# Paired heads in scores and values, a group normalisation kept in transposed layout, and a longer planned time for GpSimd's inverse roots

## The chip, the cores and the metric

The kernel runs on one core of a Trainium2 chip. Its time is the device time of one execution in microseconds (us). Three executions took 18460.33, 18463.09 and 18468.82 us; the median, 18463.09 us, is the time before.

A core has TensorE (PE in the profile; its weight loads are PEld), VectorE (DVE), ScalarE (ACT), GpSimd (POOL) and SyncE (SP), whose queue here issues all DMAs. Every engine works through its own instruction stream in order and waits on semaphores for the others.

## What is computed

32 audio sequences of 160000 samples are cut into 313 frames of 512 samples (S = 313, width 512) and turned by a cosine transform. One layer follows: an attention part and a feature part, each behind a layer norm and added to its input.

```
h = frames @ dct.T                                  # 32 x 313 x 512
X = layernorm(h)
Q, K = xpos(X @ W_Q), xpos(X @ W_K);  V = X @ W_V   # 8 heads of 64
p = softmax(Q @ K.T) * gamma_h ** |n - m|
Y = p @ V
Yn = per head: (Y - mean) * rsqrt(var + 1e-5), then * gn_weight + gn_bias
h = h + (silu(X @ W_G) * Yn) @ W_O
X = layernorm(h)
theta = X[..., None, :] / (1 + |W|) + B             # 256 x 512 angles for each frame
h = h + silu(sum_d(cos(theta) * a_cos) @ P_cos + sum_d(sin(theta) * a_sin) @ P_sin)
```

The sines and cosines are read from a table of 4096 angles in the reference; the kernel rounds the angle to the same 4096 steps and lets ScalarE compute the sine.

## The kernel before

**The feature part** is the bulk. In `ffn_round`, sequences go through it in pairs; up to four pairs form a ring, and each pair stays for 8 rounds of 32 features. `STARTS` lists the round in which each of the 16 pairs joins: pair 0 at round 0 alone, pair 1 at round 4, pair 2 at 7, pair 3 at 9, pair 4 at 11, and so on; from round 11 on the ring mostly holds three or four pairs, at the end one. A slot is 24 feature-by-sequence parts (7512 columns): VectorE makes the indices (L620, one instruction for each feature and 128 dimensions over all sequences of the ring, then L629 and L636 over the slot), ScalarE takes two sines of each slot (L644, tile `trig`, 2 buffers), TensorE sums them over the dimensions with one-hot weights of 32 columns in four column groups (L666). With one pair in the ring a slot needs 12 instructions on L620, with four pairs 3.

**The attention part** (`attention`) prepares a sequence for the ring. The frames of a sequence lie in NT = 3 overlapping tiles of N = 105 rows (`ROW0` = 0, 104, 208). Sequences 0 and 1 are prepared side by side in two sets of buffers, A and B, before the first feature round. From then on set A alone prepares the others, one after the other, beside the feature rounds, and also serves `output`. Each set has one PSUM tile `W` of four banks.

The steps of one attention are:

- `rows` (L288, 512-wide products), `copy`, `layernorm` (its inverse root is `rsqrt`: a seed on VectorE, L230 and L233, and three Newton steps of four instructions on GpSimd, L239 to L242; its result is used in L263), `transposed` (L275).
- `rows` for V into `x.h`, `rotary` for two heads at a time (`columns`, L303; L368 and L371 on VectorE; `x.qk` holds two heads in partitions 0 to 63 and 64 to 127).
- `scores`, one head at a time: three matmuls (L382) into banks 0, 1 and 2, one maximum over 105x939 (L390), one subtraction (L393).
- `exps` on ScalarE. With eng = "DVE" the sums of the exponentials follow on VectorE; with eng = "ACT" ScalarE accumulates them. "ACT" is used for sequences 0 and 1 and where the ring has one pair or none.
- For each head: the transpose of the exponentials (L436, banks 0 to 2), the decay (L448, with a window of the decay table loaded into `x.u`), the product with V (L454, nine matmuls of 105x105 by 105x64 into bank 3, in three issues); after each second head the copy back into `x.h` (L468).
- The gate (`columns` into all four banks), `silu` on ScalarE out of them (L478).
- The group normalisation in frame-by-frame layout: squares (L486 on ScalarE or L489 on VectorE), sums over each head of 64 (L494), L496 to L499 for the sums of the softmax, `rsqrt`, L503, the product (L506), then the transposes (L275), weight and bias (L517), the product with the gate (L522).
- `rows` with W_O, the residual (L525), `layernorm`, `transposed`, `copy`, and the store of the normalised sequence, transposed, to DRAM (L533). The feature rounds load it from there (L604).

**The order of the instructions** is made by `Plan`. Every step is added with a key, an engine, a planned duration and what it reads and writes. `emit` simulates the engines with these durations (300 ns more between engines, 2500 ns for a DMA to land) and issues, on each engine, the ready step with the smallest key. Feature steps have keys that count ScalarE activations of a whole slot; an attention gets keys spread between two of these, in proportion to `SHARE`, so that it is to be ready 8 such activations ahead of the round that needs it. The planned durations fix only the order; on the chip each instruction waits for what it needs. `rsqrt` plans 7500 ns for GpSimd's part.

## Time and profile before

The profiled execution took 18458.81 us, 4.28 us under the median; its span, from the first instruction to the last, is 18457.0 us.

| what | busy us | share of the span |
|---|---|---|
| ACT, of it L644 (2758 sines) | 17389.6 | 94% |
| ACT, all else | 428.2 | 2% |
| DVE, of it L620, L636, L629 | 15012.4 | 81% |
| DVE, all else | 2176.8 | 12% |
| PE, of it L666 | 10225.0 | 55% |
| POOL, all | 1128.9 | 6% |

A busy share is an average over stages. The view by stretches, cut where the ring changes, shows which engine is full in each; it is the one to read first. The view of waits says for each engine what ended its idle time, the view of groups gives the number and mean duration of like instructions, and the timeline lists instructions in order with the idle time before them in brackets.

### The profile page before, as it was taken

Reading aid. Unit: us, or ns where it says so; the run is one execution under the profiler, and the core shown is the slowest. Engines: PE = TensorE matmul, PEld = TensorE weight load, DVE = VectorE, ACT = ScalarE, POOL = GpSimd, SP = SyncE. Lnnn points to the kernel's source line nnn. Section 1 sums busy time; section 2 is a strip of 40 time slices with the busy share of each in tenths; the row PEclk is TensorE's granted clock in tenths of the full one; section 3 lists DMA queues with packets and bytes.
Section 4 is the critical chain, followed back from the end, with each engine's and each line's share of the span. In section 5 each row is a group of like instructions: output and inputs, shape, how many; then the busy total and the mean of one; then the engine's idle time right before and its main releaser. Section 6 shows DMA issues by size and latency. Waiting matters only on the chain. (4 is left out here: it accounts for less than half of the span.)

```text
span 18457.0 us, 326424 instructions
## 1 busy us (share of the span) xinstructions
PE 14446.5 (78%) x148768; PEld 6739.2 (37%) x148768; DVE 17189.2 (93%) x11340; ACT 17817.8 (97%) x3246; POOL 1128.9 (6%) x1222
## 2 busy tenths in 40 slices
PE   8888888887887887887888788877877777766666
PEld 4443434333333333333333333333333333322222
DVE  6999999999999999999999999999999999988888
ACT  3889999999999999999999999999999999999998
POOL 0001000000000000000000000000000000000000
PEclk8999999999999999999999999999999999988888
DMA  3222122111111111111121111111111111110102
GB/s 90 75 68 63 57 66 59 54 47 58 51 41 47 59 48 51 51 43 54 47 59 46 45 51 50 56 50 55 40 46 50 40 55 49 44 39 22 38 27 59
DMA packets 605415, 946.91 MB, mean 51 GB/s; under 512 B 118880, under 2 KB 344160, under 8 KB 593792
## 3 DMA queue, kind: packets, MB, share of 16 engines
q1 hardware_dynamic: 604032, 926.03, 16.9%
q8 instruction: 1166, 19.10, 0.4%
q14 instruction: 217, 1.78, 0.0%
HBM read 821.10 MB, written 104.66 MB: 50 GB/s over the span
## 5 line engine op out<-in xcount | busy, mean ns | idle before, releaser
L644 ACT ACTIVATE trig<-ix 128x7512 f32<-128x7512 int16 (+1 forms) x2758 | 17389.6, 6390 | 324.0 <-PE pa L666 140.3
L666 PE MATMUL pa<-trig,hot 128*32 128x313 f32 x131072 | 10225.0, 465 | 3490.1 <-ACT trig L644 3446.6
L666 PEld LDWEIGHTS pa<-trig,hot 128*32 128x32 f32 x131072 | 4261.3, 118 | 9265.0 <-ACT trig L644 4673.0
L620 DVE TENSOR_SCALAR ix<-xT,f 128x2504 int16<-128x2504 f32 (+3 forms) x5504 | 6526.4, 1245 | 93.8 <-ACT trig L644 55.9
L636 DVE TENSOR_SCALAR ix<-ix 128x15024 int16<-128x15024 int16 (+4 forms) x1655 | 5582.1, 3387 | 40.7
L629 DVE TENSOR_SCALAR ix<-ix 128x7512 int16<-128x7512 int16 (+1 forms) x1379 | 2903.9, 2106 | 551.9 <-ACT trig L644 466.6
L303 PE MATMUL a_W<-a_xnT,a_ring 128*128 128x313 f32 x4896 | 1445.6, 439 | 21.6 <-DVE a_prob L368 5.8
L288 PE MATMUL a_W<-a_ring,a_u 128*105 128x512 f32 x2256 | 1089.2, 623 | 124.1 <-DMA a_u<-in_frames 49.1
L303 PEld LDWEIGHTS a_W<-a_xnT,a_ring 128*128 128x128 f32 x4896 | 884.8, 190 | 576.0 <-issue 247.1
L239 POOL TENSOR_TENSOR a_gu<-a_gr 105x24 f32<-105x24 f32 x93 | 109.8, 1180 | 9222.8 <-DVE a_gr L233 9218.0
L288 PEld LDWEIGHTS a_W<-a_ring,a_u 128*105 128x105 f32 x2256 | 368.8, 175 | 731.0 <-issue 647.9
L454 PE MATMUL a_W<-a_h,a_prob 105*105 105x64 f32 x4464 | 487.9, 264 | 135.4 <-DVE a_prob L448 135.0
L454 PEld LDWEIGHTS a_W<-a_h,a_prob 105*105 105x105 f32 x4464 | 449.6, 177 | 268.5 <-issue 141.1
L382 PE MATMUL a_W<-a_u 64*105 64x313 f32 x1488 | 463.5, 444 | 64.0 <-DVE a_prob L393 50.6
L239 POOL TENSOR_TENSOR a_lu<-a_lr 105x3 f32<-105x3 f32 x186 | 197.8, 1063 | 4617.1 <-DVE a_lr L233 4528.9
L288 PE MATMUL a_W<-a_ring,a_xnT 128*105 128x512 f32 x744 | 355.0, 614 | 10.1 <-ACT a_xnT L223 5.4
L382 PEld LDWEIGHTS a_W<-a_u 64*105 64x105 f32 x1488 | 232.0, 169 | 294.1 <-issue 91.7
L436 PE MATMUL a_W<-ident,a_prob 105*105 105x105 f32 x2232 | 300.5, 272 | 32.0 <-ACT a_prob L408 17.9
L448 DVE TENSOR_TENSOR a_prob<-a_W,a_u 105x939 f32<-105x939 f32 x248 | 280.0, 1129 | 40.3 <-PE a_W L436 34.8
L390 DVE TENSOR_REDUCE a_mx<-a_W 105x3 f32<-105x939 f32 x248 | 280.0, 1129 | 36.2 <-PE a_W L382 36.1
L436 PEld LDWEIGHTS a_W<-ident,a_prob 105*105 105x105 f32 x2232 | 244.8, 177 | 127.4 <-issue 71.2
L393 DVE TENSOR_TENSOR a_prob<-a_W,a_mx 105x939 f32<-105x939 f32 x248 | 281.7, 1136 | 8.4
(134 smaller groups left out, 3474.1 us busy)
## 6 DMA issues: line engine op xcount, KB each, us to landing
hot<-in_hot SPq DMA_DIRECT2D x1376, 128.0 KB
xT<-xT_d SPq DMA_DIRECT2D x80, 1252.0 KB
a_u<-in_decay SPq DMA_DIRECT2D x248, 260.5 KB
xT<-xT_d SPq DMA_DIRECT2D x36, 939.0 KB
a_ring<-in_proj SPq DMA_DIRECT2D x128, 256.0 KB
a_ring<-in_dct SPq DMA_DIRECT2D x124, 256.0 KB
a_ring<-wv_d SPq DMA_DIRECT2D x124, 256.0 KB
a_ring<-in_wq SPq DMA_DIRECT2D x124, 256.0 KB
```

Source lines behind the costliest of these rows:

```text
L239: nc.gpsimd.tensor_tensor(u, r, r, ALU.mult)
L288: lambda c=c, i=i, k=k, to=to: nc.tensor.matmul(x.W[:N, to, :], lhsT[:, c, ROW0[i] : ROW0[i] + N], x.ring[k], start=(c == 0), stop=(c == N ...
L303: lambda c=c: nc.tensor.matmul(x.W[:, bank, :S], w[:, c, :], x.xnT[:, c, :], start=(c == 0), stop=(c == NC4 - 1)),
L382: lambda i=i: nc.tensor.matmul(x.W[:N, i, :S], qk[r0 : r0 + DH, 0, ROW0[i] : ROW0[i] + N], qk[r0 : r0 + DH, 1, :], start=True, stop=True,),
L393: lambda: nc.vector.tensor_tensor(x.prob[:N, hd], x.W[:N, :NT, :S], m[:N].unsqueeze(2).to_broadcast((N, NT, S)), ALU.subtract),
L436: nc.tensor.transpose(x.W[:N, jj, ROW0[i] : ROW0[i] + N], x.prob[:N, a, i, ROW0[j] : ROW0[j] + N], ident[:N, :N],)
L454: nc.tensor.matmul(x.y[:N, i, (hd % 2) * DH : (hd % 2 + 1) * DH], x.prob[:N, a, jj, ROW0[i] : ROW0[i] + N], x.h[:N, jj, hd * DH : (hd + 1) ...
L620: nc.vector.tensor_scalar(ix[:, x[0], pt * r * S : (pt + 1) * r * S], now["xT", y][:, : r * S], f[:, 0, n : n + 1], f[:, 1, n : n + 1], AL ...
L629: nc.vector.tensor_scalar(ix[:, x[1], :E], ix[:, x[0], :E], float(LUT // 4), None, ALU.add)
L636: nc.vector.tensor_scalar(ix[:, i, :E], ix[:, i, :E], LUT - 1, LUT // 2, ALU.bitwise_and, ALU.bitwise_xor)
L644: nc.scalar.activation(tl[:, :E], ix[:, x[1 - k], :E], AF.Sin, bias=-PI32, scale=ANG)
L666: nc.tensor.matmul(now["pa", p][g * 32 : g * 32 + 32, :S], now["hot", hot[n // 4 * 4, c]][:, n % 4, k, :], now["trig", w][:, s0 : s0 + S], ...
```

## The change

- **Scores.** A step now takes one row tile of two heads: two matmuls, one from partitions 0 to 63, one from 64 to 127, into two banks; then a maximum and a subtraction over 105x626. Two pairs of banks alternate. There are 12 steps for a sequence in place of 8.
- **Values.** The product with V is made for a pair of heads and gives Y transposed: V (64 columns) is the stationary operand, the decayed exponentials (313 columns) move, and the two heads write partitions 0 to 63 and 64 to 127 of bank 3. Six matmuls in three issues replace eighteen in six. V is stored with other strides (`x.v`), and Y transposed takes its place (`x.yT`).
- **Group normalisation.** It stays in the transposed layout. Squares (`x.sqT`), sums over each head by 12 small matmuls with a 0/1 matrix (`of_head`, loaded for each sequence) into bank 0, two VectorE instructions for the variance, `rsqrt`, three small transposes and a copy, four matmuls with `head_w` (0/1 times the weight) that spread the factor over the 64 rows of a head, one product, and four instructions that add the bias and multiply by the gate. The twelve transposes of the old way, the reciprocal and L503 are gone.
- **Planned durations and shares.** 13000 ns for GpSimd's part of `rsqrt`; new entries in `SHARE` and `TIMES`.

```diff
-SHARE = dict(rows=5.0, copy=2.5, norm=8.0, turn=0.7, rotary=4.2, scores=3.2, exps=2.0, head=3.5,
-             pair=0.8, gate=4.1, silu=1.0, group=10.7, affine=5.5)
-TIMES = dict(rows=3, copy=5, norm=2, turn=3, rotary=4, scores=8, exps=1, head=8, pair=4, gate=1,
+SHARE = dict(rows=5.0, copy=2.5, norm=8.0, turn=0.7, rotary=4.2, scores=6.4, exps=2.0, head=3.5,
+             pair=0.8, gate=4.1, silu=1.5, group=7.0, affine=5.0)
+TIMES = dict(rows=3, copy=5, norm=2, turn=4, rotary=4, scores=4, exps=1, head=8, pair=4, gate=1,
...
+            flat = self.h.rearrange("p i d -> p (i d)")
+            self.v = flat.rearrange("p (g j d) -> p j g d", g=NC4, j=NT)
+            self.yT = flat.rearrange("p (g s) -> p g s", g=NC4)[:, :, :S]
...
-        plan.add(key, "POOL", 7500, newton, (kv,), (kr, ku))
+        plan.add(key, "POOL", 13000, newton, (kv,), (kr, ku))
...
+        def scores(g):
             key = step("scores")
+            qk, kq = x.qk[g % 2], x.k("u", g % 2)
             for i in range(NT):
+                b = (g * NT + i) % 2 * 2
+                m, km = x.mx[(g * NT + i) % 2], x.k("mx", (g * NT + i) % 2)
+                def go(i=i, b=b):
+                    for a in range(2):
+                        nc.tensor.matmul(
+                            x.W[:N, b + a, :S], qk[a * DH : a * DH + DH, 0, ROW0[i] : ROW0[i] + N],
+                            qk[a * DH : a * DH + DH, 1, :], start=True, stop=True)
+                plan.add(key, "PE", 690, go, (kq,), x.banks(b, b + 1))
+                plan.add(key, "DVE", 800,
+                         lambda b=b, m=m: nc.vector.tensor_reduce(
+                             m[:N], x.W[:N, b : b + 2, :S], AX.X, ALU.max),
+                         x.banks(b, b + 1), (km,))
+                plan.add(key, "DVE", 810,
+                         lambda i=i, b=b, m=m: nc.vector.tensor_tensor(
+                             x.prob[:N, 2 * g : 2 * g + 2, i, :], x.W[:N, b : b + 2, :S],
+                             m[:N].unsqueeze(2).to_broadcast((N, 2, S)), ALU.subtract),
+                         (km, *x.banks(b, b + 1)), probs[2 * g : 2 * g + 2])
...
+                def go(g=hd // 2, jj=jj):
+                    for b in range(2):
+                        nc.tensor.matmul(
+                            x.W[b * DH : (b + 1) * DH, 3, :S],
+                            x.v[:N, jj, g, b * DH : (b + 1) * DH],
+                            x.prob[:N, 2 * g + b, jj, :], start=(jj == 0), stop=(jj == NT - 1))
+                plan.add(key, "PE", 650, go, (*probs[hd - 1 : hd + 1], hs[hd // 2]), x.banks(3))
+            plan.add(step("pair"), "DVE", 550,
+                     lambda g=hd // 2: nc.vector.tensor_copy(x.yT[:, g, :], x.W[:, 3, :S]),
+                     x.banks(3), (hs[hd // 2],))
...
+        def tables():
+            nc.sync.dma_start(x.of_head, t["of_head"])
+            nc.sync.dma_start(x.head_w, t["head_w"])
+        plan.add(key, "SP", 2 * DMA_NS, tables, (), (room[2],))
...
+        for i in range(NT):
+            def sums(i=i):
+                for c in range(NC4):
+                    nc.tensor.matmul(x.W[:N, 0, i * H : (i + 1) * H],
+                                     x.sqT[:, c, ROW0[i] : ROW0[i] + N], x.of_head[:, c, :],
+                                     start=(c == 0), stop=(c == NC4 - 1))
+            plan.add(key, "PE", 820, sums, room, x.banks(0))
+            nc.vector.scalar_tensor_tensor(f(x.gv), f(x.sm), EPS, f(x.sm), ALU.mult, ALU.mult)
+            nc.vector.scalar_tensor_tensor(
+                f(x.gv), x.W[:N, 0, : NT * H], 1.0 / DH, f(x.gv), ALU.mult, ALU.add)
+        plan.add(key, "DVE", 480, variance, (x.k("sm"), *x.banks(0)), (x.k("gv"),))
...
+        def factors():
+            for i in range(NT):
+                nc.tensor.transpose(x.W[:H, 1, ROW0[i] : ROW0[i] + N], x.gr[:N, i, :], ident[:N, :N])
+        plan.add(step("turn"), "PE", 400, factors, (x.k("gr"),), x.banks(1))
+        plan.add(step(), "DVE", 500,
+                 lambda: nc.vector.tensor_copy(x.rT, x.W[:H, 1, :S]), x.banks(1), (room[1],))
+        key = step("turn")
+        for c in range(NC4):
+            plan.add(key, "PE", 610,
+                     lambda c=c: nc.tensor.matmul(x.W[:, c, :S], x.head_w[:, c, :], x.rT,
+                                                  start=True, stop=True),
+                     room[1:], x.banks(c))
+        key = step("affine")
+        plan.add(key, "DVE", 1460,
+                 lambda: nc.vector.tensor_tensor(x.sqT, x.yT, x.W[:, :, :S], ALU.mult),
+                 (*hs, *x.banks(0, 1, 2, 3)), room[:2])
...
+                     lambda c=c: nc.vector.scalar_tensor_tensor(
+                         x.u[:, c, :], x.sqT[:, c, :], gnb[:, c : c + 1], x.u[:, c, :],
+                         ALU.add, ALU.mult),
```

## The prediction

> **What bounds the kernel now.** I read the busy times first, then the stretches, then the waits inside the stretch that loses most, then the timeline of the start.
>
> ```profile
> PE 14446.5 (78%) x148768; PEld 6739.2 (37%) x148768; DVE 17189.2 (93%) x11340; ACT 17817.8 (97%) x3246; POOL 1128.9 (6%) x1222
> ```
>
> ACT is the bound: 17817.8 of 18457.0 us. The change touches nothing of L644, and of ACT's other work only the squares of four or five sequences (105x1536 becomes 128x1252). So all that can be won is ACT's idle time, 639 us. The stretches, cut at the first sine, at the rounds in which the ring grows to two and to four pairs, and behind the last attention, say where it lies (columns: PE, PEld, DVE, ACT and POOL busy, PE's granted clock, DMA):
>
> ```profile
> 0.00:326.80 326.80, 261.49 (x992) 168.66 (x992) 145.23 (x180) 51.32 (x125) 19.99 (x82) 0.79 0.36 103
> 326.80:1018.70 691.90, 555.53 (x5153) 284.42 (x5154) 641.62 (x758) 588.21 (x201) 46.58 (x76) 0.90 0.26 75
> 1018.70:3536.50 2517.80, 2081.58 (x20609) 1011.85 (x20607) 2428.92 (x1817) 2390.49 (x457) 221.13 (x229) 0.93 0.21 60
> 3536.50:16343.00 12806.50, 10158.58 (x106416) 4712.32 (x106416) 12147.38 (x7186) 12739.73 (x2131) 841.17 (x836) 0.94 0.17 49
> 16343.00:18457.00 2114.00, 1389.31 (x15600) 561.90 (x15600) 1826.06 (x1403) 2048.04 (x335) 0.00 (x0) 0.88 0.13 37
> ```
>
> Length less ACT busy: 275.5 us idle in the start, 103.7 in rounds 0 to 3, 127.3 in rounds 4 to 10, 66.8 in the long middle, 66.0 at the end. The start is sequences 0 and 1 alone, with PE the fullest engine. In the next two stretches DVE is the fullest (93% and 96%), since L620 needs 12 or 6 instructions for a slot. After that ACT is full and attention is hidden. ACT's waits from the first sine to 3536.5, and DVE's in the same window (total, times, longest):
>
> ```profile
> ACT trig L644 <- PE pa L666: 101.7, 59, 7.0
> ACT trig L644 <- DVE ix L636: 100.5, 39, 20.1
> DVE a_h L263 <- POOL a_lr L242: 21.0, 14, 3.4
> DVE a_h L506 <- POOL a_gr L503: 11.9, 6, 2.6
> DVE ix L620 <- DMA xT<-xT_d: 10.2, 1, 10.2
> ```
>
> DVE and PE share the blame about equally. DVE stands still 33 us for Newton steps issued too early: planned 7.5 us, they took 12.4 to 13.0 us from round 6 on, 6 to 12 us before that, and only 3.2 to 5.1 us in the start.
>
> **The change part by part.**
>
> *Packing on PE.* Does a matmul on partitions 0 to 63 run beside one on 64 to 127? The old kernel shows it by accident, where B's head 0 meets A's head 1:
>
> ```profile
> 93.93 0.51 PE L382 MATMUL b_W<-b_u 64*105 64x313 f32 x1
> 93.96 0.42 PE L382 MATMUL a_W<-a_u 64*105 64x313 f32 x1
> 94.28 1.48 PE L382 MATMUL b_W<-b_u 64*105 64x313 f32 x5
> ```
>
> The first two start 0.03 us apart; otherwise records come 0.30 us apart (a matmul here is two records). L666 shows the same for column groups: 48 records of 0.46 us in 3.37 us. So a pair costs what one matmul costs, about 0.61 us at full clock (six records in 1.82 us); bounded above by 1.22, no overlap. I take 0.61. Per sequence: scores 24 x 0.61 = 14.6 becomes 7.3; values 8 heads x 1.85 (18 records of L454 at full clock) = 14.8 becomes 12 x 0.61 = 7.3. Added: 12 sums at 0.21 (L454's, 1.85/9) = 2.5 and four spreads = 2.4; three transposes for twelve save about 1.0. Net 10.9 us less PE.
>
> *DVE per sequence.* Scores: 8 x (1.130 + 1.136) = 18.1 becomes 24 instructions of 626 columns; L371 (626 columns, 0.811) prices them: 19.5. Group: squares 1.75 (eng DVE only), L494 1.75, L496 to L499 0.84, L506 1.76, L517 4 x 0.60, L522 1.46 = 9.96; now squares 1.46 (L522's row), two small 0.36, copy 0.48 (L683's shape), product 1.46, four of 313 columns at 0.60 = 6.2. Copies of pairs: 4 x (0.555 - 0.478) = 0.3 less. Net 2.7 us less (2.4 where ACT squares).
>
> *Start.* The two score phases (88 to 117 and 133 to 161.5, 28.5 us each) alternate PE and DVE on one set of banks. With two sets DVE is the bound: 12 x 2 x 0.811 + 2.3 for a rotary = 21.8. Gain 0 to 14, I take 12. The head phase, 159 to 238, is PE's: 70.7 us busy at a clock of 0.58. Here a pair of heads costs 2 x (1.87 + 3.44) = 10.6 us at half clock, 2 x (1.03 + 1.85) = 5.8 at full. New: at half 2 x 1.87 + 3.46 = 7.2 (L382's three at half clock), at full 2 x 1.03 + 1.82 = 3.9. Eight pairs: 85 (79 seen, as the clock rose at 225.7) become 58 or 31: 21 to 48 less. Transposes stay and half clock is the nearer row; but exponentials of B (11 us) then end later than PE could start, so I take 25.
>
> *The new chain.* Squares, sums and Newton used to run beside gate and silu. Now the sums need bank 0, which silu has to empty first. For A silu ended at 248.0; from there sums 2.5, small ones 0.8, Newton 3.6, transposes and copy 0.9, spreads 2.4, product 1.5, four times 0.6, and 8 handovers of 0.2 give 263.7 for a gate product that was ready at 258.4. B adds its turn behind A: 5 to 10 late, I take 9. Start: 12 + 25 - 9 = **28** (10 lost to 55 won).
>
> *Rounds 0 to 3* (sequences 2 and 3): DVE 5 us less; POOL stalls there 5 us; scores with two sets of banks need fewer turns behind L666 and L636 when they are late, but the new chain adds turns (sums, factors, spreads on PE; silu behind a sine of 6.4). PE was idle 36 us at L454 for L448, which stays. The last 20 us wait, for seq 3's last norm, store and load, stays too unless the attention comes earlier. I take **18** (10 lost to 40 won).
>
> *Rounds 4 to 10* (some six sequences): DVE 6 x 2.7 = 16; POOL stalls 28, of which the plan of 13 should leave 6; PE 66 us lighter of 2082, against 47 us of ACT's waits for it. I take **32** of 127 (0 to 60).
>
> *The rest:* ACT is full; 31 us of its waits on L666 and a few order effects: **7** (20 lost to 20 won). If DVE's lighter load had no shortage to meet, as here, it would be worth nothing.
>
> *Small things:* two loads of 16 KB for each sequence on SP, behind the last head's data by their place in the order; SP issues one in 0.33 us (L217), beside the gate; without that cover the sums would wait for a landing, about 4 us by the load of xT at 1003.0 that ended DVE's wait at 1007.2. The memset is planned longer, not changed.
>
> Sum: 18458.8 - 28 - 18 - 32 - 7 = 18373.8. That execution lies 4 us under the median, so I say **18376**.
>
> *A rule against it.* The Trainium skill ("TensorEngine Tiling (Array Packing)", Key Properties) says that a change of tiling mode drains TensorE. The trace has such a change at 5699.38: L303 with 128 columns starts 0.07 us before the last L666 in groups of 32 ends, so no drain shows. As an estimate by this rule, a drain of one matmul (0.43 us) at some 24 new borders would add 10 us of PE to each sequence and undo the saving; by the row nothing is added.
>
> *A rule for the start.* "TensorE: Matmul & The Clock Gate" (Part 4) says transposes do not count as busy for the clock. That fits 0.58 granted at 70.7 of 79 us busy. By it the clock would stay low while transposes are over half of PE's work, the 21 end.
>
> **The rivals.**
>
> *The packing gives nothing* (0.07): pairs of f32 matmuls run one after the other. Then PE gains 14.6 - 14.6, 14.8 - 14.6, less 3.9 for the group. Start: scores 8, heads 0, chain -9; rounds 0 to 3: 5; later 25 from DVE and POOL. 18463 - 29 = 18434. Against it: the three lines at 93.93.
>
> *The gain is eaten by order* (0.09): new durations shuffle the streams, the start wins 20 and the rest nothing: 18443. For it: ACT's "issue" waits of 30 us that follow no rule.
>
> *Slower* (0.10): the serial chain makes sequence 3 late for round 4, and the later ones with it. In rounds 0 to 3 silu waits behind a sine (6.4), sums and spreads each behind an L666 of 3.4 to 5.3, planned Newton adds 5.5 twice where the real one takes 6 to 9: 25 us for each of two sequences, plus 9 in the start, with 18 from DVE gone: it decides when the chain costs more than the scores save, some 20 us for each. 18463 + 50 - 12 = 18501. For it: round 4 already waited 20.1 us for L636, behind sequence 3. Against it: DVE was busy 93% there, so throughput, not latency, set most of it.
>
> **How the numbers follow.** Forecast 0.74, rivals 0.07, 0.09, 0.10. A measurement here can tell 0.2%, 37 us, from no change: under 18426 is faster. The two middle rivals lie inside the band, near its lower edge; what they give to the faster side, the forecast's tail gives back. Of the rest, the slower rival and a 0.01 tail go to slower: faster 0.74, same 0.15, slower 0.11. The parts' ends sum to 18288 and 18503; all at one end is unlikely, so 18300 to 18445, which takes in the two middle rivals. The forecast's own range is 18315 to 18425.
>
> **What would show it.** The first L644 near 299 us instead of 326.8; L382 records in pairs; the head phase nearer 55 us than 79; DVE's waits for POOL below 10 us up to round 10; round 4 starting about 46 us earlier; the long middle within 20 us of its length. Wrong would be: a first sine after 320, L454's successor without overlap, or silu and gate products that end later in each attention and move the store (L533) of sequence 3 past its old 999 us.

## The result and the profile after

The changed kernel takes 18535.9 us (median of six executions, 18521.3 to 18544.3), against 18465.6 us for the kernel before on the same chip (18460.3 to 18470.2): a ratio of 1.0037, 95% interval 1.0026 to 1.0047. It is 70 us slower, where 87 us less were forecast, and it lies outside the forecast's 18300 to 18445. Its profiled execution took 18534.3 us, with a span of 18532.6 us. In the code after, the sines are L662, their sums L684, the indices L638, L647 and L654.

The work itself became less, nearly as priced. The busy times after:

```profile
PE 14245.2 (77%) x146432; PEld 6364.6 (34%) x146432; DVE 17092.4 (92%) x11500; ACT 17821.3 (96%) x3246; POOL 1329.0 (7%) x1190
```

VectorE lost 96.8 us, 3.0 for each of 32 sequences (2.7 forecast). TensorE without the sums of the sines went from 4221.5 to 3919.7 us, 9.4 for a sequence (10.9 forecast). But GpSimd has 200 us more on fewer instructions, and ScalarE, with the same work, stands still for 711 us instead of 639. The stretches, cut at the same rounds as before:

```profile
0.00:324.20 324.20, 231.97 (x846) 124.05 (x846) 139.00 (x192) 51.06 (x124) 18.43 (x80) 0.82 0.35 104
324.20:1021.10 696.90, 555.88 (x5008) 265.80 (x5009) 634.78 (x766) 587.52 (x201) 46.06 (x74) 0.88 0.26 75
1021.10:3539.30 2518.20, 2025.49 (x20169) 940.83 (x20168) 2411.79 (x1848) 2389.70 (x457) 277.21 (x233) 0.93 0.21 60
3539.30:16416.10 12876.80, 10030.47 (x104810) 4469.38 (x104810) 12080.86 (x7295) 12744.39 (x2131) 987.30 (x804) 0.93 0.16 49
16416.10:18532.60 2116.50, 1401.39 (x15600) 564.53 (x15600) 1825.99 (x1403) 2048.66 (x335) 0.00 (x0) 0.87 0.13 37
```

The first three stretches are as long as before to within 5 us each: nothing was won. The fourth, in which ScalarE is full, is 70.3 us longer, of the 75.6 by which the two spans differ; that is nearly the whole loss. ScalarE's waits there, before and after (total, times, longest):

```profile
ACT trig L644 <- PE pa L666: 29.5, 14, 4.3
...
ACT trig L644 <- DVE ix L636: 2.5, 4, 1.3
```

```profile
ACT trig L662 <- PE pa L684: 79.6, 43, 5.7
...
ACT trig L662 <- DVE ix L654: 15.5, 10, 4.7
```

So TensorE, with less work, delivers the sums late. Some of what it waits for in this stretch, besides the sines:

```profile
PE a_W L391 <- DVE a_mx L396: 75.1, 32, 4.6
...
PE a_W L293 <- DMA a_u<-in_frames: 45.4, 8, 7.7
PE a_W L517 <- POOL a_gr L247: 41.3, 15, 4.7
```

The first and the last line are new: the matmul of a score step waits for a maximum (before, it waited for a subtraction, 17.0 us), and the transposes of the factors wait for GpSimd. The wait for frames was there before, with 26.1 us. TensorE works in order, so the sums of a sine stand behind each. Each of the two new ones is a suspect, and a third is the longer plan. From 326.8 to 3536.5 us before, VectorE waited 33 us for GpSimd. After:

```profile
DVE a_prob L400 <- PE a_W L391: 23.5, 20, 1.6
...
DVE a_prob L520 <- PE a_W L517: 11.2, 7, 3.1
DVE a_h L268 <- POOL a_lr L247: 10.6, 13, 3.4
```

The waits for GpSimd fell to 10.6 us, nearly as forecast (below 10). But the two lines on L391 and L517 are 34.7 us together, and in all VectorE stood idle for 168.5 us of these two stretches, against 139.2 before: waits for TensorE took more than the place of those for GpSimd.

**The scores.** The start, instruction by instruction (start, duration, and in brackets the idle time and what ended it):

```profile
102.52 0.80 DVE L396 TENSOR_REDUCE b_mx<-b_W 105x2 f32<-105x626 f32 x1
103.37 1.38 PE L391 MATMUL b_W<-b_u 64*105 64x313 f32 x4 [1.49 <-DVE b_mx L396]
104.79 0.81 DVE L400 TENSOR_TENSOR b_prob<-b_W,b_mx 105x626 f32<-105x626 f32 x1 [1.48 <-PE b_W L391]
```

The maximum at 102.52 reads two banks. The matmul at 103.37 is that of the next step and writes the other two, yet it waits for this maximum; and the subtraction at 104.79, whose own sums had been there before the maximum, waits for that matmul. `W` is one tile, and in these rows the accesses to it come in the order in which they were emitted, whichever banks they touch. The planned order knows single banks and lets the matmul go out between the maximum and the subtraction. So the two sets of banks work as one, with two handovers in each step that the plan doesn't know.

**The roots.** One group normalisation in the long stretch:

```profile
8870.43 1.49 POOL L244 TENSOR_TENSOR a_gu<-a_gr 105x24 f32<-105x24 f32 x1 [290.64 <-DVE a_gr L238]
...
8884.99 4.07 DVE L654 TENSOR_SCALAR ix<-ix 128x15024 int16<-128x15024 int16 x1
8885.12 4.01 POOL L244 TENSOR_TENSOR a_gu<-a_gr 105x24 f32<-105x24 f32 x1
8889.22 0.23 POOL L245 TENSOR_TENSOR a_gu<-a_gu,a_gv 105x24 f32<-105x24 f32 x1
...
8890.12 0.69 PE L517 MATMUL a_W<-ident,a_gr 105*8 105x105 f32 x3 [4.66 <-POOL a_gr L247]
8890.74 5.93 PE L684 MATMUL pa<-trig,hot 128*32 128x313 f32 x48
...
8896.80 6.47 ACT L662 ACTIVATE trig<-ix 128x7512 f32<-128x7512 int16 x1 [2.06 <-issue]
```

A GpSimd instruction of 105x24 takes 0.23 us while VectorE stands, and as long as VectorE's index instruction while one runs (4.01 beside 4.07). Twelve of them took 19.6 us here. TensorE stood 4.66 us and its sums came late, ending at 8896.67. ScalarE stood 2.06 us and began 0.13 us behind them; the profile names no releaser for this wait ("issue"), so that it waited for the sums is read from the times. Over the whole run the median of the first of the four instructions of a Newton step (three steps for each of 31 roots of the group in buffers A) went from 0.84 to 1.40 us; first the kernel before, then after (minimum, median, maximum in ns):

```profile
L239 POOL TENSOR_TENSOR a_gu<-a_gr x93: 225/837/4022, 240.4 to 16127.0; 105x24 f32<-105x24 f32 x93
```

```profile
L244 POOL TENSOR_TENSOR a_gu<-a_gr x93: 224/1404/4020, 235.2 to 16244.1; 105x24 f32<-105x24 f32 x93
```

So the "12.4 to 13.0 us" that the prediction read as the time of the Newton steps was made by the plan of 7.5: VectorE ran out of other work, stood still for the result, and let GpSimd finish fast. With 13 planned, VectorE is given index work in the meantime; from round 11 on the group's twelve instructions then took 18.4 us (median) instead of 12.9. The plan did not do that alone: with 13 planned they took 13.6 us beside the old scores (e3) and 13.9 in the kernel before (e2).

### The profile page after: what moved, and what is told of

Read it like the earlier page. It is cut to its first block, busy times and chain, and to the rows that moved or that the text cites. A ratio compares the mean times of both kernels' runs of the same rounds, so it can differ in the third digit from the quotient of the medians.

```text
span 18532.6 us, 322232 instructions
## 1 busy us (share of the span) xinstructions
PE 14245.2 (77%) x146432; PEld 6364.6 (34%) x146432; DVE 17092.4 (92%) x11500; ACT 17821.3 (96%) x3246; POOL 1329.0 (7%) x1190
## 5 line engine op out<-in xcount | busy, mean ns | idle before, releaser
L662 ACT ACTIVATE trig<-ix 128x7512 f32<-128x7512 int16 (+1 forms) x2758 | 17394.3, 6391 | 401.1 <-PE pa L684 226.9
L684 PE MATMUL pa<-trig,hot 128*32 128x313 f32 x131072 | 10325.5, 469 | 3612.9 <-ACT trig L662 3559.9
L684 PEld LDWEIGHTS pa<-trig,hot 128*32 128x32 f32 x131072 | 4288.8, 119 | 9527.0 <-ACT trig L662 4789.1
L638 DVE TENSOR_SCALAR ix<-xT,f 128x2504 int16<-128x2504 f32 (+3 forms) x5504 | 6526.4, 1245 | 121.7 <-ACT trig L662 88.8
L654 DVE TENSOR_SCALAR ix<-ix 128x15024 int16<-128x15024 int16 (+4 forms) x1655 | 5583.0, 3388 | 41.9
L647 DVE TENSOR_SCALAR ix<-ix 128x7512 int16<-128x7512 int16 (+1 forms) x1379 | 2906.8, 2108 | 608.8 <-ACT trig L662 522.0
L308 PE MATMUL a_W<-a_xnT,a_ring 128*128 128x313 f32 x4896 | 1456.2, 441 | 44.5 <-DVE a_prob L400 15.6
L293 PE MATMUL a_W<-a_ring,a_u 128*105 128x512 f32 x2256 | 1094.4, 623 | 138.4 <-DMA a_u<-in_frames 70.3
L293 PEld LDWEIGHTS a_W<-a_ring,a_u 128*105 128x105 f32 x2256 | 365.4, 175 | 744.3 <-issue 631.9
L443 PE MATMUL a_W<-ident,a_prob 105*105 105x105 f32 x2232 | 289.8, 274 | 134.3 <-DVE a_prob L455 105.2
L391 PE MATMUL a_W<-a_u 64*105 64x313 f32 x1488 | 274.1, 472 | 151.0 <-DVE a_mx L396 118.1
L400 DVE TENSOR_TENSOR a_prob<-a_W,a_mx 105x626 f32<-105x626 f32 x372 | 301.2, 810 | 87.9 <-PE a_W L391 64.3
L293 PE MATMUL a_W<-a_ring,a_xnT 128*105 128x512 f32 x744 | 353.5, 613 | 10.4 <-DVE a_xnT L230 5.7
L396 DVE TENSOR_REDUCE a_mx<-a_W 105x2 f32<-105x626 f32 x372 | 298.2, 802 | 49.8 <-PE a_W L391 33.3
L443 PEld LDWEIGHTS a_W<-ident,a_prob 105*105 105x105 f32 x2232 | 238.4, 178 | 280.5 <-issue 136.4
L455 DVE TENSOR_TENSOR a_prob<-a_W,a_u 105x939 f32<-105x939 f32 x248 | 279.9, 1129 | 18.4 <-PE a_W L443 11.5
L466 PE MATMUL a_W<-a_prob,a_h 105*64 105x313 f32 x1488 | 239.6, 452 | 67.4 <-DVE a_prob L455 66.4
L374 DVE TENSOR_TENSOR a_prob<-a_W,a_prob 128x1252 f32<-128x1252 f32 x124 | 180.6, 1456 | 44.8 <-PE a_W L370 38.9
L428 DVE TENSOR_REDUCE a_sm<-a_prob 105x6 f32<-105x1878 f32 x108 | 220.0, 2100 | 0.0
```

The lines of the kernel that those rows point to most:

```text
L293: lambda c=c, i=i, k=k, to=to: nc.tensor.matmul(x.W[:N, to, :], lhsT[:, c, ROW0[i] : ROW0[i] + N], x.ring[k], start=(c == 0), stop=(c == N ...
L308: lambda c=c: nc.tensor.matmul(x.W[:, bank, :S], w[:, c, :], x.xnT[:, c, :], start=(c == 0), stop=(c == NC4 - 1)),
L396: lambda b=b, m=m: nc.vector.tensor_reduce(m[:N], x.W[:N, b : b + 2, :S], AX.X, ALU.max),
L400: lambda i=i, b=b, m=m: nc.vector.tensor_tensor(x.prob[:N, 2 * g : 2 * g + 2, i, :], x.W[:N, b : b + 2, :S], m[:N].unsqueeze(2).to_broadca ...
L443: nc.tensor.transpose(x.W[:N, jj, ROW0[i] : ROW0[i] + N], x.prob[:N, a, i, ROW0[j] : ROW0[j] + N], ident[:N, :N],)
L455: nc.vector.tensor_tensor(x.prob[:N, a], x.W[:N, :NT, :S], w3, ALU.mult)
```

## The experiments

Four causes were held apart: N (the longer plan for GpSimd), S (the new score steps cost by themselves), G (the group's roots now feed TensorE), and later F (the false order within `W` is S's cause). Each time below is a median, with its ratio to the kernel before, measured beside it (18459 to 18470 us), and the 95% interval. The runs are called e1 to e18, in the order in which they were made.

**One part undone, or one part alone**

```diff
-        plan.add(key, "POOL", 13000, newton, (kv,), (kr, ku))
+        plan.add(key, "POOL", 7500, newton, (kv,), (kr, ku))
```

> The changed kernel with one number put back: 7500 ns planned for GpSimd's Newton steps in place of 13000. In the changed kernel they lasted 18.4 us (median, group normalisation, behind 3540 us) against 12.9 before. Theory N (the longer plan fills VectorE with index work, under which the Newton steps take still longer, and what follows stands in TensorE's stream): most of the 70 us come back, 18460 to 18490 us; the Newton steps fall to about 13 us and VectorE waits for them again. Theory S (the score steps make TensorE wait for VectorE): little changes, 18510 to 18540. Theory G (the factors of the group now feed TensorE straight from GpSimd): with a shorter plan TensorE stands longer at L517, so the same or slower, 18530 to 18580.

e1: 18499.1 us, 1.0022 (1.0012 to 1.0032): 37 us of the 72 come back (18535.9 was 72 over the 18463.9 measured beside this run), between the ranges of theory N and theory S. The two profiles differ by 43 us, 27.7 of them ahead of round 4 and 12.8 in the long stretch.

```diff
-        plan.add(key, "POOL", 7500, newton, (kv,), (kr, ku))
+        plan.add(key, "POOL", 13000, newton, (kv,), (kr, ku))
```

> The kernel before with that one number alone: 13000 in place of 7500. Theory N: slower by itself, 18490 to 18530 us, Newton steps of 16 to 19 us in the middle. Theories S and G: no loss, VectorE's stalls for GpSimd (121 us over the run) go, 18430 to 18470.

e2: the kernel before with this one number takes 18495.0 us, 1.0017 (1.0008 to 1.0025), 31 us more. Of these the profile shows 11.6 in the start, where the steps take 3 to 5 us and 13 planned put sequence A's work behind B's, and 9.5 in rounds 0 to 3. The long stretch is only 6.8 us longer, and there the Newton steps took 13.9 us in the group and 15.0 in the norms (12.9 and 12.6 before), not the 16 to 19 of theory N. So the longer plan costs by itself, but mostly ahead of round 4, and not by the index work that theory N named.

In the next, the changed kernel has the score steps of before (one head, three banks), with their entries in `SHARE` and `TIMES`; then the reverse, the kernel before with the new ones.

```diff
-            for i in range(NT):
-                b = (g * NT + i) % 2 * 2
...
-                        nc.tensor.matmul(
-                            x.W[:N, b + a, :S], qk[a * DH : a * DH + DH, 0, ROW0[i] : ROW0[i] + N],
...
+                    lambda i=i: nc.tensor.matmul(
+                        x.W[:N, i, :S], qk[r0 : r0 + DH, 0, ROW0[i] : ROW0[i] + N],
```

> The changed kernel with the scores of before (one head at a time, three banks, one maximum and one subtraction of 939 columns). Of the 69 us that ScalarE lost in the long middle, 36 us follow a gap of TensorE at the scores or at the rotary behind them. Theory S: 18490 to 18505 us, and TensorE's 75 us at L391 for the maximum go. Theories N and G: 18525 to 18545, as the scores only swap one VectorE-bound chain for another.

e3: 18483.8 us, 1.0011 (1.0002 to 1.0019): 52 us come back, some more than theory S had.

> The kernel before with the new scores alone. Theory S: 18495 to 18510 us, with new gaps of TensorE at the scores. Theories N and G: 18440 to 18470; TensorE is 7 us lighter and VectorE 1.4 us heavier for each sequence.

e4: 18514.7 us, 1.0026 (1.0016 to 1.0037): 51 us more than before. N and S are both real, and no theory with a single cause is left. The rest would be a gain of 14, if costs added up.

**What is left: values and group alone.** The kernel of the third run, with 7500 ns.

> The changed kernel without the new score steps and with 7500 ns for the Newton steps: only the packed values and the new group normalisation are left of the change. If the costs add up (all parts together +72 us against before, scores 52, the longer plan 34 by the four runs so far), these parts alone gain 14: 18450 +- 12. If the parts cost only in company (a theory of order: every shuffle of the streams costs), it comes out at 18463 to 18485. By the first theory the long middle (before: 12247.5 us from round 12 to round 35) stays within 15 us.

e5: 18484.1 us, 1.0016 (1.0007 to 1.0024). They did not add up: these parts alone cost 24 us, and the longer plan beside them nothing (18483.8 with it). Its long stretch is 56 us longer than before's. For each of ScalarE's waits over 0.25 us from 4095 to 16400 us I looked for the longest idle time of TensorE in the 16 us ahead that was not one of L683's own. Before, these waits sum to 59 us, and none follows a step that GpSimd released directly. Here they sum to 106, of which 43 follow L516, the transposes of the factors (L517 in the kernel after), and 36 follow L293 (16 of it behind the load of frames, 14 behind that of `in_proj`; before, L288 had 30). Before, 19 us followed transposes that wait for a product of VectorE with a root (L506, L263), so the roots stood ahead of TensorE there too, one step removed. The lines of that stretch, before and here:

```profile
PE a_W L275 <- DVE a_h L506: 33.7, 9, 5.2
```

```profile
PE a_W L516 <- POOL a_gr L247: 56.5, 20, 4.3
```

The same count for the changed kernel itself gives 126 us: 60 follow L293 (38 of it the load of frames), 32 a score step or a rotary that waits for VectorE, and only 12 the factors, L517.

**The false order, told to the plan**

```diff
-                plan.add(key, "PE", 690, go, (kq,), x.banks(b, b + 1))
+                plan.add(key, "PE", 690, go, (kq,), x.banks(0, 1, 2, 3))
...
-                         x.banks(b, b + 1), (km,))
+                         x.banks(0, 1, 2, 3), (km,))
```

Likewise in the subtraction. In a second kernel, every access to `W` declares the whole tile:

```diff
-            return [self.k("W", x) for x in i]
+            return [self.k("W", 0)]
```

Both keep GpSimd's roots, with 7500 ns.

> The changed kernel with 7500 ns, and its score steps now declare all four banks of the PSUM tile to the order (the instructions are the same, only their order can move). Theory F (false order: a matmul into one pair of banks waits on the chip for the maximum of the other pair, and the subtraction for that matmul, because accesses to one tile are kept in the order in which they are emitted; the planned order knows nothing of it): against 18499 with 7500 ns alone, some 40 of the scores' 52 us come back, 18450 to 18465, and TensorE's waits of L391 for L396 in the long middle fall from 64 us to under 25. Theory T (twelve turns between TensorE and VectorE cost more than eight, however they are planned): 18490 to 18505.

> The changed kernel with 7500 ns, and every access to W, not only those of the scores, declares the whole tile to the order. Theory F: the heads have the same fault (values and their copy in bank 3 against transposes and decay in banks 0 to 2), so it is at least as fast as the scores' declaration alone: 18435 to 18460. Rival: the order then sees the heads as one serial chain and spreads nothing; with the chain as long on the chip as it was, no more comes than from the scores (18450 to 18470), or the attention comes late in the start and round 4 is 20 us later (18480).

e6 and e7: 18496.2 us (1.0021, 1.0012 to 1.0030) and 18491.1 us (1.0018, 1.0009 to 1.0027): theory F missed. The waits of L391 for L396 did go (63.9 us from 4094 to 16400 us, no such line with the declaration), but those of L517 for GpSimd rose from 53.0 to 60.1 us. The first sine did come at 303.8 instead of 316.5 us, but rounds 0 to 3 gave it back (698.4 instead of 676.9 us), and the long stretch stayed.

**The roots on VectorE**

```diff
-                nc.gpsimd.tensor_tensor(u, r, r, ALU.mult)
+                nc.vector.tensor_tensor(u, r, r, ALU.mult)
...
-        plan.add(key, "POOL", 7500, newton, (kv,), (kr, ku))
+        plan.add(key, "DVE", 2500, newton, (kv,), (kr, ku))
```

First with the values and group parts alone:

> The values and group parts alone, with the twelve Newton instructions on VectorE instead of GpSimd. VectorE then never waits for GpSimd (43 us for the norm and 53 us of TensorE for the group's roots in the long middle of the changed kernel with 7500 ns), and pays some 12 x 0.2 = 2.4 us for each of about 95 inverse roots, 230 us in all, against 330 us in which it waits for ScalarE in the long middle. Theory N (the time of the Newton steps is made by what VectorE does meanwhile, so it can't be planned): 15 us less than the values and group parts alone, 18425 to 18445, most of it in the long middle. Rival: in rounds 0 to 10 VectorE is full, so 25 roots there cost 60 us against stalls of 33: 18450 to 18475, with round 11 some 20 us later.

e8: 18408.1 us, 0.9975 (0.9964 to 0.9985): 76 us less, where 15, or 18425 to 18445, were expected; of it 76.2 in the long stretch. Of the waits of ScalarE attributed as above, 34 us are left, none behind L516. An instruction of the group's roots now takes 0.183 us whatever runs beside it:

```profile
L244 DVE TENSOR_TENSOR a_gu<-a_gr x93: 182/183/185, 227.3 to 16109.0; 105x24 f32<-105x24 f32 x93
```

Then with all parts, next in the kernel before, and last with the values and group parts where only the group calls for VectorE:

```diff
-    def rsqrt(plan, key, val, r, u, kv, kr, ku):
+    def rsqrt(plan, key, val, r, u, kv, kr, ku, eng="POOL"):
...
-        plan.add(key, "POOL", 7500, newton, (kv,), (kr, ku))
+        plan.add(key, eng, 7500 if eng == "POOL" else 2500, newton, (kv,), (kr, ku))
...
-        rsqrt(plan, key, x.gv[:N], x.gr[:N], x.gu[:N], x.k("gv"), x.k("gr"), x.k("gu"))
+        rsqrt(plan, key, x.gv[:N], x.gr[:N], x.gu[:N], x.k("gv"), x.k("gr"), x.k("gu"), "DVE")
```

> The changed kernel with the twelve Newton instructions on VectorE (planned 2500 ns); nothing on GpSimd is waited for. Theory P (a wait of TensorE's or VectorE's own queue for GpSimd is what the change lost by; the longer plan and the group's factors are one cause, since both work through the Newton steps): all of the 72 us and more comes back, 18415 to 18435, the scores costing 0 to 15 us beside the values and group parts with the same roots (18408). Theory S (the new score steps cost 50 us by themselves): 18450 to 18470.

e9: 18466.6 us, 1.0002 (0.9993 to 1.0011): 69 of the 72 us come back, but not the more that theory P had: beside the kernel without the new scores (18408.1) they cost 58 us again, as theory S had it.

> The kernel before with the twelve Newton instructions on VectorE. If the values and group parts are a gain once nobody waits for GpSimd: 18425 to 18445, slower than those parts with the same roots (18408). If the whole gain of that kernel is that of the roots: 18400 to 18412. If VectorE's waits for GpSimd were harmless before (120 us in all, half of them in the stretch in which ScalarE is full): 18455 to 18470.

e10: 18441.4 us, 0.9988 (0.9979 to 0.9997). Values and group are a gain of 33 us where nobody waits for GpSimd.

> The values and group parts alone (18484), with the Newton steps on VectorE in the group normalisation only; the two norms keep GpSimd with 7500 ns. Theory G (TensorE's transposes of the factors, L516, stand in its queue behind GpSimd's roots, and the sums of the sines behind them; 43 of 106 us of ScalarE's idle time from round 12 to 35 are due to it): 35 to 50 us come back, 18435 to 18450, and ScalarE's idle time in that stretch falls from 111 to some 65 us. Rival (VectorE's waits for the norms' roots, L268, cost as much): 18460 to 18475.

e11: 18419.4 us, 0.9976 (0.9967 to 0.9986): the group's roots alone bring 65 of the 76 us, and the long stretch is 65 us shorter (12797.1 us). This is theory G's direction, GpSimd's result ahead of a TensorE step, but more than its 35 to 50: of ScalarE's 106 us of waits 41 are left, none behind the factors. The 43 that followed L516 are gone, and 22 more that the count had not put down to it. The norms' roots, which VectorE waits for, are worth the small rest at most.

**The false order again, with the roots out of the way**

> The changed kernel with the Newton steps on VectorE and the score steps declaring all four banks. Theory F (false order in the scores, seen in the start alone: the first sine came 12.7 us earlier with the declaration): 5 to 15 us less than the changed kernel with the roots on VectorE and no declaration, and its first sine near 295. Rival: the order pays the 13 us back in rounds 0 to 3, as it did with the roots on GpSimd (676.9 became 698.4): within 5 us of it.

e12: 18406.8 us, 0.9970 (0.9959 to 0.9981): with all roots on VectorE the declaration brings 60 us, all that the scores had cost, where theory F had seen 5 to 15. Of it 13 us lie in the start, 19 in rounds 4 to 10 and 26 in the long stretch. The first sine comes at 297.3 us. Its score phase:

```profile
92.48 0.81 DVE L396 TENSOR_REDUCE a_mx<-a_W 105x2 f32<-105x626 f32 x1
92.61 1.38 PE L391 MATMUL b_W<-b_u 64*105 64x313 f32 x4 [0.18 <-DVE b_prob L400]
93.33 0.81 DVE L400 TENSOR_TENSOR a_prob<-a_W,a_mx 105x626 f32<-105x626 f32 x1
94.05 0.80 DVE L396 TENSOR_REDUCE b_mx<-b_W 105x2 f32<-105x626 f32 x1
94.19 1.38 PE L391 MATMUL a_W<-a_u 64*105 64x313 f32 x4 [0.20 <-DVE a_prob L400]
94.89 0.81 DVE L400 TENSOR_TENSOR b_prob<-b_W,b_mx 105x626 f32<-105x626 f32 x1
```

The same instructions, but the order now alternates sequences A and B, whose tiles are two: VectorE has no gap, and is the bound.

**Is the cause the scores' own, and what does a shuffle do?**

> The kernel before with the new score steps, which declare all four banks to the order. Undeclared they made it 51 us slower. Theory F (unplanned waits between TensorE and VectorE): at least 35 of the 51 us come back, 18455 to 18480, and TensorE's waits for the maximum in the long middle (39 us) all but vanish. Rival (the declaration helps only where the roots are on VectorE, so it is not the scores' own cause): 18495 to 18515.

e14: in the kernel before, with GpSimd's roots as they were, the declaration brings the new score steps from 18514.7 to 18460.6 us (1.0002, 0.9993 to 1.0010), the time before. That is theory F's forecast, in a second kernel. TensorE's waits for maxima in the stretch from 4094 to 16400 us, without the declaration and with it (there no such line is left, only waits for an earlier subtraction, which were 6.8 us without it):

```profile
PE a_W L385 <- DVE a_mx L390: 39.0, 22, 4.9
```

```profile
PE a_W L385 <- DVE a_prob L394: 25.5, 19, 2.3
```

The direct test, the two pairs of banks in two tiles, was not run. The control is a planned number alone:

```diff
-        plan.add(step(), "POOL", 500, lambda: nc.gpsimd.memset(x.h[0:1, : NT - 1, :], 0.0), (), hs)
+        plan.add(step(), "POOL", 2000, lambda: nc.gpsimd.memset(x.h[0:1, : NT - 1, :], 0.0), (), hs)
```

> The kernel before with the planned duration of one memset for each sequence raised from 500 to 2000 ns (as the change does): the instructions are the same, the order may shift. A control of what a shuffle alone does. If the causes named (roots, scores) are real and not luck of the order: within 15 us of before, 18447 to 18477. If any shuffle costs 20 to 50 us (the kernel before being a lucky order): 18480 to 18510.

e13: 18458.1 us, 0.9999 (0.9990 to 1.0008). The planned number left the order of the instructions as it was, so this shows repeatability only: the first sine of its profile came at 333.3 us, against 326.8, and stretches of single profiles are good to some 7 us there. Two kernels that do shuffle it:

```diff
-    WAIT = 300.0
+    WAIT = 350.0
```

> The kernel before, with 350 instead of 300 ns planned for a handover between engines; the same instructions in an order of which over a third of VectorE's and TensorE's lines are shifted. If order by itself is worth little: within 15 us of before, 18445 to 18475. If the order of before was a lucky one: 18480 to 18510, and then effects under some 40 us in the other runs prove nothing.

> The same with 250 ns. If order by itself is worth little: 18445 to 18475; if the order of before was a lucky one: 18480 to 18510.

e17 and e18: 18474.3 us with 350 and 18476.1 us with 250 (both 1.0003, 0.9994 to 1.0012): 4 and 6 us more than before, inside an interval of 17 either way. So the order of before was no lucky one among these three. But these shuffles are small: 851 and 586 of VectorE's 11340 instructions stand at another place in its stream, against 2732 of 11596 between e4 and e14 and 2420 of 12652 between e9 and e12. A change of order of that size is e6, where 2431 of 11500 moved and 3 us came of it. The 50 to 76 us of the scores and roots are well above all three; the 24 us of e5 are less sure. And for one stretch a shuffle does count: with 350 the first sine came at 314.9 us, 11.9 earlier than before, with nothing else changed.

**Could it be better still?** Two forms with the scores declared: the declaration for every access to `W`, with all roots on VectorE; and only the group's roots there, with the norms on GpSimd.

> The changed kernel with the Newton steps on VectorE, and every access to W (not the scores alone) declares the whole tile. If the heads (values and copy in bank 3 beside transposes in banks 0 to 2) have the fault of the scores: 10 to 25 us less than the declaration of the scores alone (18407), 18382 to 18397. If not: 18402 to 18415.

> The changed kernel with the score steps declaring all four banks, the group's roots on VectorE and the norms' on GpSimd with 7500 ns. If the norms' roots on GpSimd are harmless now that they feed VectorE only: within 8 us of the kernel with all roots on VectorE (18407), rounds 4 to 10 some 8 us shorter (VectorE is full there and is spared 24 instructions for each sequence), the long middle as much longer. If VectorE's 45 us of waits for the norms' roots in the long middle count: 18420 to 18440.

e15 and e16: 18427.3 us (0.9982, 0.9973 to 0.9991) and 18418.7 us (0.9978, 0.9970 to 0.9987). The first is slower than either expectation had it. The heads do have such waits (VectorE's copy L472 behind the transposes L443: 23.8 us in e12 from 4094 to 16400 us, no such line here), but telling the order of them costs 20 us instead of winning any. The second lies between its two expectations; rounds 4 to 10 are as long with the norms on GpSimd as without (2512.2 and 2513.2 us), so VectorE's spared instructions there brought nothing. The best version is the change with its roots on VectorE and its scores declared, 18406.8 us, level with the kernel that has the old scores (18408.1).

## Why the prediction was wrong

The stretches of the profiles, in us (the long one runs from round 11 to the last attention):

| kernel | start | rounds 0 to 3 | 4 to 10 | long | end |
|---|---|---|---|---|---|
| before | 326.8 | 691.9 | 2517.8 | 12806.5 | 2114.0 |
| after | 324.2 | 696.9 | 2518.2 | 12876.8 | 2116.5 |
| before, new scores (e4) | 332.4 | 684.3 | 2547.4 | 12826.2 | 2114.0 |
| the same, declared (e14) | 311.3 | 689.0 | 2530.1 | 12809.2 | 2115.2 |
| values and group (e5) | 315.3 | 685.5 | 2509.4 | 12862.5 | 2114.1 |
| the same, group's root on VectorE (e11) | 315.5 | 680.2 | 2506.7 | 12797.1 | 2112.4 |
| all, roots on VectorE (e9) | 310.5 | 677.2 | 2532.4 | 12832.3 | 2115.9 |
| the same, declared (e12) | 297.3 | 673.7 | 2513.2 | 12806.5 | 2113.1 |

Of the four terms, 28 us in the start became 2.6, 18 in rounds 0 to 3 became a loss of 5.0, 32 in rounds 4 to 10 a loss of 0.4, and 7 in the rest a loss of 72.8, nearly all in the long stretch. (The sum itself is 2 us off: 85 from the median is 18378, not 18376.) The prediction had "After that ACT is full and attention is hidden"; there attention was not hidden.

- **The step that failed first: "With two sets DVE is the bound: 12 x 2 x 0.811 + 2.3 for a rotary = 21.8."** Two sets of banks in one tile worked as one set. The last subtraction of the scores came at 168.4 us, not earlier than before (160.4). Once the order knew it (e14), it came at 153.8, 6.6 us earlier, and the first sine 15.5 us earlier, where 12 were forecast; as the shuffle with 350 moved the first sine by 11.9, the size of the term is not shown. The same error stands in "scores with two sets of banks need fewer turns". In the long stretch it cost instead of gaining nothing (26 us from e12 to e9, 17 from e14 to e4). The kernel before had the evidence: VectorE's copy out of bank 3 waited for a transpose into banks 0 to 2 (its view of waits, from 4094 to 16400 us), which no data asks for:

```profile
DVE a_h L468 <- PE a_W L436: 40.6, 35, 3.1
```

- **The second: "POOL stalls 28, of which the plan of 13 should leave 6."** The stalls of VectorE did fall, from 33 to 10.6 us. But the time of the Newton steps is no constant, and the longer plan lengthened them (18.4 us for 12.9 in the changed kernel). As a single change it costs 31 us (e2), 21 of the 30 in its profile ahead of round 4: the prediction did not ask what a plan of 13 us does in the start, where it had read 3.2 to 5.1.
- **The third: the new chain was priced for the start and for rounds 0 to 3, and the long stretch at "7 (20 lost to 20 won)".** The prediction listed "sums, factors, spreads on PE" as turns, in rounds 0 to 3. It didn't say what is queued behind L517 on TensorE in the long stretch: the sums of the sines. Undoing that wait in the group alone is worth 65 us with the old scores and 7500 ns (e5 to e11). In the changed kernel only 12 us of ScalarE's waits directly follow L517, but all roots on VectorE, which also undoes the longer plan, bring 69 there (18535.9 to e9's 18466.6).
- **Right: the packing.** Matmuls of the two halves run side by side (four records in 0.78 us at 99.40), and the last pair of heads was copied 50.8 us after the scores ended, instead of 77.9: 27 us less, 25 forecast. That the two agree is partly luck. The prediction took half clock as the nearer row, at which eight pairs alone are 58 us; the whole phase took 51.3, at a granted clock of 0.81 (0.59 before), full from 188.6 us on (before from 225.7). By the rule that it quoted, the clock "would stay low while transposes are over half of PE's work"; here the transposes had 19.6 us and the values 17.4, and the clock rose. The 27 us were given back behind it. With 13 us planned, sequence B's factors went out at 253.62, behind A's W_O rows, though B's last Newton instruction had ended at 242.8; and A's last norm at 278.87, 8.7 us after its root.
- **Right in sum, but for another kernel: the start and rounds 0 to 3.** In e12 the first sine comes at 297.3 us (near 299 was forecast), and round 4 at 971.0, 47.7 us earlier (46 forecast). But e12 has its roots on VectorE, which alone brought round 4 of the kernel before 20.4 us forward (e10, 998.3); so the agreement is in part luck.
- **Wrong in every run: the 32 us of rounds 4 to 10.** VectorE did lose 17 us of work there, as priced (16), and its waits for GpSimd fell from 28 to 7 us, as forecast. But its idle time rose from 88.9 to 106.4 us: it now waited for TensorE, 18.6 us for the score steps (L400 for L391) and 8.1 for the factors (L520 for L517). In no run did the stretch become shorter by more than 15.6 us (e3, with the old scores).

The change's three parts can't be read one at a time: the longer plan costs 31 us alone, 37 in the changed kernel and nothing beside the values and group parts alone; the undeclared scores cost 51, 58 and 52 us, but only 15 beside these parts with 7500 ns. The rival that ended on the slower side named a serial group chain that makes sequence 3 late for round 4. Round 4 came 2.4 us later only; so its mechanism was not this one, though it did name spreads that stand behind the sums of the sines.

Open are three things. In the changed kernel the largest part of ScalarE's waits in the long stretch, 60 of 126 us, follows L293, and its 38 us behind the load of frames (14 before) were not taken up by any run. The declaration brought 60 and 54 us in two kernels and only 3 where GpSimd's roots feed TensorE with 7500 ns planned (e6); why the one hides the other wasn't traced step by step. And e12's last seven rounds with attention, 28 to 34, are 22 us longer than those of e8 (3483.3 against 3461.5), without a line in the views that says why.

## What to carry to other kernels

Read a helper engine's duration together with what its neighbours do in that time: a time measured while the others wait for it is a product of the plan, and a longer plan can lengthen it. Before a step is moved to another engine, name what stands behind it in that engine's queue; here a result that VectorE could wait for cheaply was put ahead of the engine that feeds the bound. An order planned by hand must know the dependences that the built program really keeps (in these traces whole tiles, not banks); a matmul that waits for a reader of other banks shows the difference in the trace.

## What the runs showed of the hardware

GpSimd's small instructions of 105x24 took about as long as the index instruction of VectorE that they met: 0.23 us alone, 1.4 to 2.2 us beside L638, L647 and L654, 4.01 beside one of 4.07, with ends 0.07 us apart (8889.13 and 8889.06). The Trainium skill ("SBUF — State Buffer", Who interferes with whom) says that VectorE in a 2-port mode, which `tensor_scalar` can enter, contends with GpSimd for a shared port pair: whoever issues first holds it for the whole instruction, and the other is fully blocked. The trace agrees with such a block, with the rows at 8884.99 (a `tensor_scalar`) and 8885.12; in which mode VectorE ran, no row says. VectorE itself lost nothing on average: its index instruction of 128x15024 took 4.07 us (mean of 1075) in the changed kernel and the same in e8, where GpSimd has no roots. On VectorE the same instruction took 0.183 us: GpSimd by itself, at 0.23, is little slower for this shape; the rest of its time came with VectorE's instructions.
